# Tile outputs summed six jobs behind their request instead of four, with 15 buffers for them instead of 11

## The chip, the cores and the metric

The kernel runs on one core of one Trainium2 chip. The metric is the device time of one execution in microseconds (us). The kernel before takes 1431.49 us, the median of three runs (1430.09 to 1435.99). The profile was taken from a further execution.

## What is computed

Four layers are applied to 4096 rows of 128 numbers (16 sequences of 256). Each layer adds to its input an attention-like part and a feed-forward part of the normalised input. The change touches the end of layer 0 and the beginning of layer 1. Layer 0's feed-forward part is a mixture of eight experts, cut here to what matters:

```
logits = xn @ gate_w.T;  probs = softmax(logits)
tk_probs, tk_idx = top_k(probs, 2);  tk_probs /= sum(tk_probs) + EPS
out = swiglu(xf, shared)
for e in range(8):
    out = out + w[:, e:e+1] * swiglu(xf, Wg[e], Wu[e], Wd[e])    # w: the two weights, else 0
x = x + ssm(xn) + out
xn = layernorm(x)            # then layer 1: causal attention with 16 heads, and a SwiGLU
```

So each row needs the outputs of two experts, weighted and added.

## The kernel before

**Layout.** The 4096 rows are eight blocks `X[0..7]` of four tiles of 128 rows; a tile has a row in each partition. `HALVES` are the blocks 0 to 3 and 4 to 7; within a half a tile has the number n from 0 to 15.

**Routing and scattering.** Rows are sorted by expert through DRAM. Each row gets two slots in a tensor `XS` of 40 tiles of 256 slots. POOL (GpSimd) writes the rows there with 64 indirect DMAs (L449), 32 for each half: "scatters" below. The first half's rows fill only the tiles below `FIRST` = 24; the second half fills up tiles and takes the rest.

**The jobs.** The loop at L797 takes 40 jobs, k = 0 to 39, one for each tile of 256 slots. Job k fetches weights and slots six jobs ahead on SP's queue (L618, L625), transposes the slots on PE (L636) and evicts them on ACT (L638), two jobs ahead. One job ahead it does the two up-projections (PE tiles `sg` and `su`), SiLU on ACT (L648) and their product on DVE (L649). Then it does the down-projection (PE tile `sy`), evicts it on DVE (L660) and stores it to `YS` in DRAM on SP's queue (L661). PE, ACT, DVE, SP and POOL run in the order in which this block is written (`manual_schedule`); POOL's instructions that are written after the block are merged into its queue when the program is built. The order of the jobs is such that after job 23 all slots of the first half have their outputs.

**Fetching and summing.** From job 24 on, `fetch_outputs(0, n)` (L665) asks for the outputs of one tile of the first half: two indirect DMAs on POOL (L668), "gathers" below, into two tiles `yk` of 64 KB. The dictionary `asked` (L795) says which job asks for which n: 24 for 0 and 1; 25 for 2; 26 for 3; 27 for 4 and 5; 28 for 6; 29 for 7; then one a job up to n = 11 at job 33. `combine(0, n)` (L673) multiplies both by the row's weights and adds them to `X` with two DVE instructions (L678). It stands at the end of the job four behind the request (L811), after that job's L660. All `yk` tiles go round 11 buffers, so that gather number j (0 to 63 in order) waits for the sum that read gather j - 11.

**The first norms.** When output 7 is summed, blocks 0 and 1 are complete, and `norm_steps` (L179) for them is put on the list `norms`. Each job from then on takes one step: statistics of block 0; statistics of block 1 and, on POOL, the scale (`inv_std`, L123 and L124); normalisation of block 0 (DVE, L148); its transposition (PE, L157) and copy (ACT, L194); the same two steps for block 1. When output 11 is summed, the norm of block 2 is appended. What is left when the jobs end is done then (L819).

**Behind the jobs.** The outputs n = 12 to 15 of the first half and all 16 of the second form the list `left` (L827). Six of them are requested at once (12 gathers). The rest follow in `rest()` (L831), a generator that layer 1's attention calls between its own steps: each call sums two outputs and requests two more, and after every fourth output it runs the norm of the block. The second half's outputs need all of `YS`, so the last store too. POOL also issues the load of `pk1i`, weights of layer 1 (L89).

**Layer 1's attention** (`attention`, L850) starts with `project` of block 0, whose matmuls (PE tiles `pq`, `pk`, `pv`) stand behind the last of those norms in PE's order, then the scores `sc`, their maxima on DVE (L952), the weights `se` and the context `av`.

Of the kernel before, what the change touches and what calls it, by code (L numbers as in the profile page):

```python
# [10 lines left out]
F32 = mybir.dt.float32  # L11
# [8 lines left out]
P = 128  # L20
B, S, D = 16, 256, 128
# [34 lines left out]
def program(ctx: ExitStack, tc: tile.TileContext, x, consts, consts0, rows, pk0, w0s, w0e, pk1, pk1i, pk2, pk3, out):  # L56
    nc = tc.nc

    cp = ctx.enter_context(tc.tile_pool(name="keep", bufs=1))
# [119 lines left out]
    def norm_steps(pool, blocks, layer, into=None):  # L179


        n = len(blocks) * NT
        mv = pool.tile([P, n, 2], F32, tag="mvs", name=f"mv{layer}_{blocks[0]}")
        for k, i in enumerate(blocks):
            stats(pool, X[i], mv[:, k * NT : (k + 1) * NT, :], f"st{layer}_{i}")
            if i == blocks[-1]:
                r = inv_std(pool, mv, n, f"r{layer}_{blocks[0]}")
            yield
        for k, i in enumerate(blocks):
            t = into(i) if into else pool.tile([P, NT, D], F32, tag="xn", name=f"xn{layer}_{i}")  # L190
            normalise(t, X[i], mv, r, k * NT)
            yield
            ps = transpose4(t, f"xnT{layer}_{i}")
            nc.scalar.copy(xT[i], ps)  # L194
            yield


    with early, banks(8, 0), tc.tile_pool(name="l0", bufs=2) as sp:
# [21 lines left out]
        for spans in (((0, E), (E + SURE, E + MOST)), ((E + MOST, E + MOST + 8), (E + MOST + 8, TILES))):  # L220
            fills.append([])
            for a, b in spans:
                n = (b - a) * SLOTS // P
# [220 lines left out]
        def at_rows(idx):  # L444
            return bass.IndirectOffsetOnAxis(ap=idx, axis=0)
# [158 lines left out]
        def fetch_weights(k):  # L604
            p = jobs[k] - E
            w = live.setdefault(k, {})
            t = sp.tile([P, 8, 128], F32, tag="blk", name=f"we{k}", bufs=8)
            w["w"] = t[:, 0:6, :]
            for a, b in ((0, SURE), (SURE, WHOLE)):
                if p != a:  # L610
                    continue
                _, values = nc.values_load_multi_w_load_instructions(
                    rows_of[0:1, a:b], engines=[mybir.EngineType.SP], min_val=0, max_val=(E - 1) * P,
                    skip_runtime_bounds_check_because="an expert's number, at most the last one's, times 128",
                )
                experts.update(zip(range(a, b), values))
            of = w0e[bass.ds(experts[p], P), :] if p >= 0 else w0e[(p + E) * P : (p + E + 1) * P, :]
            nc.sync.dma_start(out=w["w"].rearrange("p a b -> p (a b)"), in_=of)  # L618

        def fetch_slots(k):  # L620
            t = jobs[k]
            needs = scatters[0] if k < SURE else scatters[0] + scatters[1]
            assert len(scatters[0]) == 2 * HN and len(scatters[1]) == 2 * HN
            xs = live.setdefault(k, {})["xs"] = sp.tile([P, SLOTS // P, D], F32, tag="xs", name=f"xs{k}", bufs=8)
            d = nc.sync.dma_start(  # L625
                out=xs, in_=XS[rows_in(t), :].rearrange("(t p) d -> p t d", p=P)
            )
            for s in needs:
                tc.add_manual_dep(d.ins, s.ins.name, sync, reason="slots filled")
            return d  # L630

        def turn_slots(k):
            v = live[k]
            ps = bank(f"xsT{k}")
            for t in range(SLOTS // P):
                nc.tensor.transpose(ps[:, t * P : (t + 1) * P], v["xs"][:, t, :], ident)  # L636
            v["xT"] = sp.tile([P, SLOTS], F32, tag="xsT", name=f"xsT{k}", bufs=3)
            nc.scalar.copy(v["xT"], ps[:, 0:SLOTS])  # L638

        def up_slots(k):  # L640
            v = live[k]
            pg, pu = bank(f"sg{k}"), bank(f"su{k}")
            for c in range(2):
                mm(pg[:, c * SLOTS : (c + 1) * SLOTS], v["w"][:, c, :], v["xT"])
            for c in range(2):
                mm(pu[:, c * SLOTS : (c + 1) * SLOTS], v["w"][:, 2 + c, :], v["xT"])
            h = v["h"] = sp.tile([P, 2 * SLOTS], F32, tag="hs", name=f"hs{k}", bufs=3)
            nc.scalar.activation(h, pg, AF.Silu)  # L648
            nc.vector.tensor_tensor(h, h, pu, ALU.mult)  # L649

        def down_slots(k):
            v, to = live.pop(k), jobs[k]
            py = bank(f"sy{k}")
            for t in range(SLOTS // P):
                for c in range(2):
                    o = c * SLOTS + t * P
                    mm(py[:, t * P : (t + 1) * P], v["h"][:, o : o + P], v["w"][:, 4 + c, :], c == 0, c == 1)

            ys = (sp, cp)[k >= NJ - 2].tile([P, SLOTS // P, D], F32, tag="ys", name=f"ys{k}", bufs=3 if k < NJ - 2 else 2)
            nc.vector.tensor_copy(ys, py[:, 0:SLOTS].rearrange("p (t d) -> p t d", d=D))  # L660
            return nc.sync.dma_start(out=YS[rows_in(to), :].rearrange("(t p) d -> p t d", p=P), in_=ys)  # L661

        fetched = {}

        def fetch_outputs(hf, n):  # L665
            for k in range(2):
                y = fetched[hf, n, k] = cp.tile([P, D], F32, tag="yk", name=f"yk{hf}_{n}_{k}", bufs=11)
                nc.gpsimd.indirect_dma_start(  # L668
                    out=y, out_offset=None, in_=YS[0 : FIRST * SLOTS, :] if hf == 0 else YS[:, :],
                    in_offset=at_rows(slots[:, hf, k, n : n + 1]),  # L670
                )

        def combine(hf, n):  # L673
            i = HALVES[hf][n // NT]
            x = X[i][:, n % NT, :]
            for k in range(2):
                m = top[k][:, hf * HN + n : hf * HN + n + 1]
                nc.vector.scalar_tensor_tensor(x, fetched.pop((hf, n, k)), m, x, ALU.mult, ALU.add)  # L678

        def mixed(i):  # L680
            po = bank(f"po0_{i}")
            for t in range(NT):
                mm(po[:, t * P : (t + 1) * P], yT[:, t % 2, 2 * i + t // 2, :], mix, t == 0, t == NT - 1)
            xf = X[i].rearrange("p t d -> p (t d)")
            nc.vector.tensor_tensor(xf, xf, po, ALU.add)
# [101 lines left out]
        with tc.manual_schedule(engines=ordered | {mybir.EngineType.Pool}):  # L787
            for k in range(AHEAD):
                fetch_weights(k)
                fetch_slots(k)  # L790
            for k in range(2):
                turn_slots(k)
            up_slots(0)
            norms = []
            asked = {FIRST: (0, 1), FIRST + 1: (2,), FIRST + 2: (3,), FIRST + 3: (4, 5), FIRST + 4: (6,), FIRST + 5: (7,)}  # L795
            asked.update({FIRST + 6 + n: (8 + n,) for n in range(4)})
            for k in range(NJ):  # L797
                if k + AHEAD < NJ:
                    fetch_weights(k + AHEAD)
                for n in asked.get(k, ()):  # L800
                    fetch_outputs(0, n)
                if k + AHEAD < NJ:
                    fetch_slots(k + AHEAD)
                if k + 2 < NJ:
                    turn_slots(k + 2)
                if k + 1 < NJ:
                    up_slots(k + 1)
                if k % 2 == 0 and 1 <= k // 2 <= NBLK:
                    mixed(k // 2 - 1)
                stored = down_slots(k)  # L810
                for n in asked.get(k - 4, ()):  # L811
                    combine(0, n)
                    if n == 7:
                        norms.append(norm_steps(sp, (0, 1), 1, again))
                    if n == 11:
                        norms.append(norm_steps(sp, (2,), 1, again))
                if norms and next(norms[0], True):
                    norms.pop(0)
            for f in norms:  # L819
                for _ in f:  # L820
                    pass
# [6 lines left out]
        for hn in left[:6]:  # L828
            fetch_outputs(*hn)

        def rest():  # L831
            waiting = left[6:]
            for k in range(0, len(left), 2):
                for hn in left[k : k + 2]:
                    combine(*hn)
                    if waiting:
                        fetch_outputs(*waiting.pop(0))
                yield
                done = left[k + 1]
                if done[1] % NT == NT - 1:  # L840
                    yield from norm_steps(fp, (HALVES[done[0]][done[1] // NT],), 1)
# [818 lines left out]
```

## Time and profile before

| | us |
|---|---|
| median of the runs | 1431.49 |
| the profiled execution | 1435.41 |
| its span, first to last instruction | 1433.6 |
| PE busy (share of the span) | 1267.3 (88%) |
| DVE busy | 774.9 (54%) |
| ACT busy | 561.4 (39%) |
| POOL busy | 344.8 (24%) |
| the 64 gathers, from first to last | 287.5 to 495.4 |
| the 40 jobs' last eviction (L660) begins | 343.66 |
| mean granted clock of TensorE | 0.94 |

The lines of a timeline have the start, the duration, the engine, the line of the kernel, the operation, the tile written and the tiles read, shapes, and in brackets the engine's idle time before and what ended it. PE is the matmul, PEld the load of weights. Groups of the page have the number of instructions behind an x, then busy time and mean duration in ns, then the idle time before them.

### The profile page before, as it was taken

To read this page: it belongs to the slowest core of one execution; us is meant where nothing else is said; L and a number is where in the kernel's file an instruction comes from. 1 tells how busy PE (TensorE), PEld (TensorE's weight loads), DVE (VectorE), ACT (ScalarE), POOL (GpSimd) and SP (SyncE) were. 2 spreads that over 40 slices of the span, in tenths; PEclk is the share of its full clock that TensorE was granted. 3 is DMA by queue.
4 is the path that set the end of the run, shared out by engine and by line. 5 is a ranking of instruction groups with operands and counts; after the bars stand their busy time and mean duration, and the time that the engine had idled before them with its cause. 6 is when DMAs were issued, how large, how long until landed. Compare 5 with 4: busy or idle time off the path is not lost.

```text
span 1433.6 us, 27549 instructions
## 1 busy us (share of the span) xinstructions
PE 1267.3 (88%) x11630; PEld 812.5 (57%) x11630; DVE 774.9 (54%) x1587; ACT 561.4 (39%) x868; POOL 344.8 (24%) x512
## 2 busy tenths in 40 slices
PE   3733699987889999999899999999998999999896
PEld 2512469975555566666545555455555666667434
DVE  7422254435756677767446433554337666567267
ACT  4400122323334544453334433444234555553552
POOL 2456100064312100001012211222112444434012
PEclk9656799998889999999999999999999999999998
DMA  6922575874100000000000000000000000000002
GB/s 195 306 88 74 154 238 170 245 208 149 53 13 16 11 2 3 2 2 2 1 0 0 1 0 0 1 1 0 0 0 2 2 2 2 2 2 2 2 1 59
DMA packets 66731, 72.12 MB, mean 50 GB/s; under 512 B 7344, under 2 KB 57008, under 8 KB 66096
## 3 DMA queue, kind: packets, MB, share of 16 engines
q1 hardware_dynamic: 61936, 60.62, 13.7%
q0 software_dynamic: 4240, 8.99, 2.0%
q8 instruction: 92, 1.51, 0.4%
q10 hardware_dynamic: 432, 0.75, 0.2%
q14 instruction: 31, 0.25, 0.1%
HBM read 52.45 MB, written 17.89 MB: 49 GB/s over the span
## 4 chain that ended last, share of the span: by engine, by line
PE 78%; DVE 12%; issue 6%; ACT 3%; another core or an unknown queue 1%; POOL 0%; DMA 0%; ACTq 0%; DVEq 0%; POOLq 0%
PE h L117 15%; PE sc L117 9%; PE se L117 7%; PE po L117 6%; PE av L117 5%; DVE M L952 4%; PE c L117 3%; PE sy L117 3%; PE sg L117 3%; PE mT L967 2%; PE su L117 2%; PE cv L117 2%; PE pq L117 2%; PE pk L117 2%; PE a L117 1%
## 5 line engine op out<-in xcount | busy, mean ns | idle before, releaser
L952 DVE TENSOR_REDUCE M<-sc 128x4 f32<-128x1024 f32 (+3 forms) x256 | 196.1, 819 | 107.6 <-PE sc L117 98.9
L117 PE MATMUL h<-h,pk 128*128 128x512 f32 x512 | 221.6, 592 | 0.0
L997 ACT ACTIVATE E<-se 128x1024 f32<-128x1024 f32 (+1 forms) x192 | 158.9, 880 | 77.3 <-PE se L117 76.9
L117 PEld LDWEIGHTS h<-h,pk 128*128 128x128 f32 x512 | 96.4, 190 | 117.2 <-issue 115.0
L1004 POOL TENSOR_SCALAR_AFFINE_SELECT E<-E 64x256 f32<-64x256 f32 x240 | 100.5, 419 | 140.5 <-ACT E L997 129.0
L117 PE MATMUL se<-Q,Km 32*128 32x256 f32 (+3 forms) x2048 | 124.0, 336 | 9.9 <-DVE M L952 6.6
L117 PE MATMUL sc<-Kp,Qm 32*128 32x256 f32 (+3 forms) x2048 | 124.3, 338 | 3.0 <-DVE M L952 1.5
L117 PEld LDWEIGHTS sc<-Kp,Qm 32*128 32x128 f32 x2048 | 94.3, 192 | 57.3 <-issue 30.7
L668 POOL DMA_INDIRECT yk<-YS,slots x64 | 61.8, 965 | 248.6 <-DMA we<-in_w0e 135.9
L117 PEld LDWEIGHTS se<-Q,Km 32*128 32x128 f32 x2048 | 88.8, 188 | 48.8 <-issue 34.9
L123 POOL TENSOR_TENSOR v_r<-mv,power 128x4 f32<-128x4 f32 (+1 forms) x23 | 5.2, 226 | 441.1 <-DVE mv L144 441.1
L1243 ACT ACTIVATE h<-h,pk 128x512 f32<-128x512 f32 x64 | 44.0, 687 | 140.8 <-PE h L117 140.7
L117 PE MATMUL cv<-toe,Z 128*32 128x128 f32 x512 | 38.1, 346 | 55.6 <-issue 49.6
L1253 DVE TENSOR_TENSOR x<-x,po 128x512 f32<-128x512 f32 x8 | 5.5, 688 | 139.2 <-PE po L117 139.2
L117 PE MATMUL av<-E,vals 128*32 128x256 f32 (+3 forms) x2048 | 77.2, 301 | 3.8 <-ACT c L1293 1.5
L1022 ACT COPY cu<-av 128x512 f32<-128x512 f32 x32 | 18.8, 586 | 143.5 <-PE av L117 130.3
L449 POOL DMA_INDIRECT XS<-xn,slots x64 | 62.1, 970 | 49.4 <-issue 34.4
L117 PEld LDWEIGHTS av<-E,vals 128*32 128x32 f32 x2048 | 52.7, 110 | 25.0 <-ACT c L1293 2.4
L117 PEld LDWEIGHTS cv<-toe,Z 128*32 128x32 f32 x512 | 23.9, 193 | 68.1 <-issue 61.7
L649 DVE TENSOR_TENSOR hs<-hs,su 128x512 f32<-128x512 f32 x40 | 27.5, 687 | 58.5 <-PE su L117 50.3
L148 DVE TENSOR_SCALAR xn<-x,mv,r 128x128 f32<-128x128 f32 x100 | 46.8, 532 | 14.2 <-POOL r L124 14.1
L117 PE MATMUL sy<-we,hs 128*128 128x128 f32 x320 | 44.2, 283 | 6.9 <-DVE hs L649 6.9
(303 smaller groups left out, 2239.8 us busy)
## 6 DMA issues: line engine op xcount, KB each, us to landing
toe<-kd SPq DMA_DIRECT2D x32, 512.0 KB
we<-in_w0e SPq DMA_DIRECT2D x40, 384.0 KB
xs<-XS SPq DMA_DIRECT2D x40, 128.0 KB
YS<-ys SPq DMA_DIRECT2D x40, 128.0 KB
pk<-in_pk SPq DMA_DIRECT2D x1, 3145.5 KB
XS<-Z SPq DMA_DIRECT2D x3, 1024.0 KB
x<-in_x SPq DMA_DIRECT2D x8, 256.0 KB
ycd<-yc SPq DMA_DIRECT2D x8, 256.0 KB
```

The source lines that it names most:

```text
L117: nc.tensor.matmul(o, l, r, start=start, stop=stop)
L148: nc.vector.tensor_scalar(dst[:, t, :], src[:, t, :], mv[:, at + t, 0:1], r[:, at + t : at + t + 1], ALU.subtract, ALU.mult,)
L449: d = nc.gpsimd.indirect_dma_start(out=XS[:, :], out_offset=at_rows(slots[:, hf, k, n : n + 1]), in_=xn[HALVES[hf][n // NT]][:, n % NT, :] ...
L649: nc.vector.tensor_tensor(h, h, pu, ALU.mult)
L668: nc.gpsimd.indirect_dma_start(out=y, out_offset=None, in_=YS[0 : FIRST * SLOTS, :] if hf == 0 else YS[:, :], in_offset=at_rows(slots[:, h ...
L952: nc.vector.tensor_reduce(dst, src, AX.X, ALU.max, negate=True)
L967: nc.tensor.transpose(ps[:, T, c * P : (c + 1) * P], negm[bl][:, c, T].rearrange("p g j k -> p (g j k)"), ident)
L997: nc.scalar.activation(E[:, 2 * n : 2 * n + 2, :], se[n][:, :, 0 : 2 * wide], AF.Exp, scale=ISQ)
L1004: nc.gpsimd.affine_select(out=d[r], in_=d[r], pattern=[[0, 2], [0, 2], [1, 64]], compare_op=ALU.is_ge, fill=0.0, base=0, channel_multiplie ...
L1022: nc.scalar.copy(cu, ps.rearrange("p (t q) -> p t q", t=2))
L1243: nc.scalar.activation(hn[:, c, :], ps, AF.Gelu, scale=W2[sn][:, c : c + 1])
L1253: nc.vector.tensor_tensor(xf, xf, po, ALU.add)
```

## The change

```diff
         def fetch_outputs(hf, n):
             for k in range(2):
-                y = fetched[hf, n, k] = cp.tile([P, D], F32, tag="yk", name=f"yk{hf}_{n}_{k}", bufs=11)
+                y = fetched[hf, n, k] = cp.tile([P, D], F32, tag="yk", name=f"yk{hf}_{n}_{k}", bufs=15)
...
                 stored = down_slots(k)
-                for n in asked.get(k - 4, ()):
+                for n in asked.get(k - 6, ()):
                     combine(0, n)
                     if n == 7:
                         norms.append(norm_steps(sp, (0, 1), 1, again))
```

The sum of each of the first twelve outputs moves from the job four behind the request to the job six behind it: outputs 0 and 1 from job 28 to job 30, output 7 from job 33 to 35, output 11 from job 37 to 39. The requests stay at jobs 24 to 33. The list `norms` gets its entries two jobs later. The tag `yk` has 15 buffers, four of 512 bytes a partition more, so that gather j waits for the sum that read gather j - 15. This holds for the outputs of `left` too, which use the same tag.

## The prediction

> **What bounds the kernel now.** I read the chain of waits first: PE holds 78% of the chain that ended last, and in the stretch that this change touches (about 287 to 370 us) it is PE matmuls of the expert jobs, broken by stalls. So I asked next for everything that touches the fetched tiles `yk`.
>
> ```profile
> L668 POOL DMA_INDIRECT yk<-YS,slots x64 | 61.8, 965 | 248.6 <-DMA we<-in_w0e 135.9
> ```
> ```profile
> who waited for it (us, times):
>   POOL yk L668: 96.8, 11
>   PEld sc L117: 0.8, 1
>   ACT hs L648: 0.4, 1
>   PE av L117: 0.3, 1
> ```
>
> The first line is the gather, 64 times, 965 ns each; with the 0.30 us between two of them in the timeline, one every 1.25 us. The second list is who waited for a gather or for the sum that frees its buffer. It is nearly all POOL waiting for a free buffer. No DVE row stands there: no sum of L678 ever waited for its tile. The tightest is output 6, fetched at 307.0 and 308.3 us and summed at 318.5, 10 us later. **So the later sum removes no wait of DVE.** What the extra buffers can move is when POOL issues gathers. The busy time by stages shows why that matters (columns: window, its length, then busy time of PE, PEld, DVE, ACT, POOL; then granted clock, DMA share, GB/s).
>
> ```profile
> 250.00:270.00 20.00, 20.00 (x134) 18.69 (x133) 8.68 (x16) 6.19 (x13) 0.00 (x0) 1.00 0.81 249
> 287.00:292.00 5.00, 5.00 (x35) 4.66 (x34) 1.80 (x3) 1.57 (x3) 3.63 (x4) 1.00 0.90 237
> 292.00:302.00 10.00, 5.10 (x29) 4.10 (x27) 1.11 (x2) 0.97 (x2) 6.87 (x8) 0.99 0.57 171
> ```
>
> Before the gathers PE is full. The first run of 11 gathers starts at 287.46; some 4 us later PE, DVE and ACT all fall to half or less, at a granted clock of 0.99 and a falling DMA share. The rows of DVE give the price (L660 evicts one job, here jobs 24 to 27):
>
> ```profile
> 286.26 0.42 DVE L660 COPY ys<-sy 128x256 f32<-128x256 f32 x1
> 289.10 0.42 DVE L660 COPY ys<-sy 128x256 f32<-128x256 f32 x1
> 293.26 0.42 DVE L660 COPY ys<-sy 128x256 f32<-128x256 f32 x1 [1.46 <-PE sg L117]
> 301.11 0.69 DVE L649 TENSOR_TENSOR hs<-hs,su 128x512 f32<-128x512 f32 x1 [7.42 <-remote]
> 303.21 0.42 DVE L660 COPY ys<-sy 128x256 f32<-128x256 f32 x1 [1.41 <-remote]
> ```
>
> A job takes 2.84 us until the gathers run, then 4.16 and 9.95. The multiplication at 301.11 waits for a matmul that PE began at 292.82; it starts when the eleventh gather ends (301.01). The same is plain in the scatter stage, the other long run of indirect DMAs (32 of them, 54.77 to 95.3 us), in PE's timeline:
>
> ```profile
> 90.33 0.37 PE L117 MATMUL cv<-toe,Z 128*32 128x128 f32 x1 [2.43 <-issue]
> 93.13 0.37 PE L117 MATMUL cv<-toe,Z 128*32 128x128 f32 x1 [2.43 <-issue]
> ...
> 100.13 1.16 PE L117 MATMUL cv<-toe,Z 128*32 128x128 f32 x16 [0.33 <-issue]
> ```
>
> One matmul in 2.8 us while the run lasts and 16 in 1.16 us after it. So a long unbroken run of gathers slows PE from about 4 us after its start until its end. I fit the price from the L660 rows. Jobs 25 to 28 (289.10 to 304.81) take 15.71 against 3 x 2.84 = 8.52: 7.2 lost, run of 13.55 us. Jobs 28 to 31 (to 315.96): 2.6 lost, run of six, 7.2 us. Jobs 31 to 34 (to 330.00): 5.5 lost, run of eight, 9.8 us, part of it a clock of 0.83 afterwards. Jobs 34 to 37 (to 339.71): 1.2 lost, 0.95 of it a wait for POOL's scale, seven gathers in twos and threes. **Price: 0.75 x (length of the run - 4 us)**, which gives 7.2, 2.4, 4.3 and 0, together 13.9.
>
> **The change, part by part.**
>
> *Twelve sums moved two jobs later.* Their 24 instructions (349 ns each) still run on DVE in the loop, which is busy 9 us in 20 there; instructions and DMA bytes stay. Cost 0; PE's jobs cover it. If that cover went, 24 x 0.35 = 8.4 us would show, before as now.
>
> *The norms follow the sums.* `norms` is appended at job 35 instead of 33 and 39 instead of 37, one step per job. Before, the first generator (six steps) ends at job 38, and only the norm of block 2 is left over. Now five steps fit, and job 39 holds the sum of output 11 and the normalisation of block 1. This lies on the path that sets the end:
>
> ```profile
> 343.66 0.42 DVE L660 COPY ys<-sy 128x256 f32<-128x256 f32 x1 [0.91 <-PE sy L117]
> 344.00 0.28 DVE L143 BATCH_NORM_STATS2 st<-x 128x6 f32<-128x128 f32 x1
> ...
> 345.77 0.20 POOL L123 TENSOR_TENSOR v_r<-mv,power 128x4 f32<-128x4 f32 x1 [6.82 <-DVE mv L144]
> ...
> 347.13 1.25 DVE L148 TENSOR_SCALAR xn<-x,mv,r 128x128 f32<-128x128 f32 x4 [1.45 <-POOL r L124]
> 347.33 1.02 POOL L668 DMA_INDIRECT yk<-YS,slots  x1 [0.24 <-issue]
> 347.62 1.29 PE L157 MATMUL xnT<-consts,xn 128*128 128x128 f32 x4 [4.00 <-DVE xn L148]
> ```
>
> PE idles 4.00 us while DVE and POOL make block 2's norm, and attention's projections stand behind that transpose. Now a sum pair (0.73, row at 333.50) and a normalisation (1.11, row at 340.70) come ahead of the row at 344.00: **+1.8**. Block 1's transpose (0.44 of PE at 342.13) leaves the loop for that idle time: **-0.4**.
>
> *POOL's place of the scale.* Behind the `v_r` row at 345.77 wait DVE's normalisation and, through it, PE. It now becomes ready 3.9 us after job 39's eviction instead of 2.0. The gathers that need all stores can start 3.0 us after it (their last semaphore wait ended at 346.62, the next gather at 347.33). If the built order puts none of them ahead, 0; if all seven, 7 x 1.25 = 8.8 less 0.9 of slack, about 8. The trace cannot say; the nearest row has the scale ahead, but there it was ready first. I take half a gather, **+0.6**.
>
> *The runs of gathers in the loop.* A gather waits for the sum of the tile 15 places back (11 before). First run: tiles 0 to 14, 18.5 us, price 0.75 x 14.5 = 10.9. Job 28 then evicts at 289.10 + 8.52 + 10.9 = 308.5 and job 30 at 314.2, where the first sums now stand (before, job 30 evicted at 314.35 too). Second run: tiles 15 to 18 at job 30, 19 and 20 at 31, 21 and 22 at 32, unbroken, 10 us: 4.5. Third: 23 to 26 at job 33, 27 and 28 at 34, 7.5 us: 2.6. Then twos: 0. Together 18.0 against 13.9: **+4.1**. Bounds: if the later runs all break up, only 10.9 is left of the 16.5 measured, -5.6; if the 17 gathers after the first run merge into one of 21 us, 10.9 + 12.9 - 13.9 = +10.
>
> The Trainium skill, SBUF — State Buffer, section "Who interferes with whom", says the reverse of my price: a DMA never contends with a compute engine, and only the port pair shared by DVE and GpSimd does. By it this term would be 0. The rows at 292 and at 90 us differ, PE being slowed most.
>
> *After the loop.* Three gathers (347.33 to 350.88) stood ahead of the tile that waited for a sum until 360.84. Now four more are free: seven, 8.75 us, price 3.6. The chain there holds PE for 1.72 + 1.13 + 1.11 + 1.41 = 5.4 of the 9 us from 348.9 to 358.0, so I count 0.6 of it: **+2.1** (bounds 0 and 3.6). In attention the gates are the same sums four tiles on, so the runs of eight at 360.8 and 391.0 stay. Of the last gathers (485.6 to 495.4) four go: 5.0 us, **-0.7**. POOL's other queue entries there (the `pk1i` load at 350.87) have 60 us to spare. SP's queue is not touched: its order and waits are the jobs'.
>
> *Four buffers more* cost space alone (4 x 512 bytes a partition).
>
> **Sum:** 1.8 - 0.4 + 0.6 + 4.1 + 2.1 - 0.7 = +7.5 us on the profiled execution's 1435.4 (span 1433.6, 1.8 around it). That run lies 3.9 above the median of the runs, 1431.5; I add the 7.5 to the median: **1439.0**.
>
> **The rivals.**
>
> *1. The runs cost by something other than their length* (the loads beside them, the number of gathers, which stays). Only the norms count: 1.8 - 0.4 + 0.6, so 1433.5. For it: the run at 360.8 to 370.7 shows no such loss. Against: the scatter stage, and jobs 34 to 37.
>
> *2. Faster: the later runs break up.* From job 30 on, POOL is let go by two tiles a job (2.5 us of gathers per 2.84 us). If the sums come that evenly, no run lasts 4 us after the first; 10.9 replaces the measured 16.5, -5.6, with +1.4 for the norms and -0.7 at the end: -5, 1426.5; 1421 to 1428 with the spread of the fit. It decides from the point where POOL's gaps after tile 18 exceed about 1 us per pair. For: pairs at 327.8 to 332.2 cost nothing visible. Against: jobs 30 and 33 release four at once.
>
> *3. Slower still: POOL's scale stands behind the gathers* (8 instead of 0.6), or the later runs merge (+10 instead of +4.1): 1443 to 1449.
>
> *4. The change does what its words say and no more:* sums had 10 us and over to spare, so this is rival 1's time.
>
> **How the numbers follow.** About 0.5% (7.2 us) is what a measurement of this kernel can tell from no change. The forecast case (1436 to 1442) gets 0.45, 0.25 of it over 1438.7 and 0.20 under. Rivals 1 and 4 (1431 to 1436): 0.20, all within. Rival 3: 0.22, slower. Rival 2: 0.13, 0.07 of it under 1424.3 and so faster. That makes faster 0.07, same 0.46, slower 0.47. The range from 1426 to 1448 leaves out half of rival 2, the end of rival 3 and what I have not thought of. The forecast case's own range is 1436 to 1442.
>
> **What would show it.** Right: the first run has 15 gathers in a row and jobs 25 to 28 take about 19.4 us; job 30 evicts near 314; the gap between the last L660 and the first projection grows from 5.0 us by about 2; seven gathers follow the last store. Wrong: jobs 25 to 28 unchanged with a longer run (then length is not the cause), any DVE wait for `yk`, or more than one gather between the last store and the scale (rival 3).

## The result, and the profile after

| | before | after |
|---|---|---|
| median of the runs, us | 1432.8 (6 runs, 1430.09 to 1437.62) | 1441.37 (6 runs, 1439.37 to 1445.23) |
| profiled execution, us | 1435.41 | 1440.46 |
| its span, us | 1433.6 | 1438.8 |
| mean granted clock of TensorE | 0.940 | 0.942 |

The ratio is 1.0055, with a 95% interval of 1.0042 to 1.0068: 8.6 us slower between the medians. The two profiled executions differ by 5.1 only, since that of before lies 2.6 above its median and that of after 0.9 below.

POOL still waits for the sums that free its buffers, and still no sum waits for its tile. The list of who waited for `yk`:

```profile
who waited for it (us, times):
  POOL yk L668: 103.0, 12
```

The first run of gathers has 15 now, from 285.5 to 304.1 us. DVE's rows beside it (L660 evicts jobs 25 to 28):

```profile
287.20 0.42 DVE L660 COPY ys<-sy 128x256 f32<-128x256 f32 x1
292.04 0.42 DVE L660 COPY ys<-sy 128x256 f32<-128x256 f32 x1 [2.13 <-PE su L117]
299.98 0.69 DVE L649 TENSOR_TENSOR hs<-hs,su 128x512 f32<-128x512 f32 x1 [7.51 <-remote]
307.00 0.42 DVE L660 COPY ys<-sy 128x256 f32<-128x256 f32 x1 [6.33 <-remote]
308.60 0.42 DVE L660 COPY ys<-sy 128x256 f32<-128x256 f32 x1
```

Jobs 25 to 28 take 21.40 us (15.72 before). The busy time in the same stretch (window, its length, PE, PEld, DVE, ACT, POOL, clock, DMA share, GB/s):

```profile
290.00:304.00 14.00, 7.56 (x39) 6.16 (x36) 1.11 (x2) 0.97 (x2) 10.65 (x12) 0.87 0.48 139
```

PE, DVE and ACT all fall, as before; only POOL is busy. The next place is behind the last job, whose eviction begins at 347.82:

```profile
348.81 1.11 DVE L148 TENSOR_SCALAR xn<-x,mv,r 128x128 f32<-128x128 f32 x4
...
350.86 1.01 POOL L668 DMA_INDIRECT yk<-YS,slots  x1 [6.03 <-DMA YS<-ys]
352.17 0.97 POOL L668 DMA_INDIRECT yk<-YS,slots  x1 [0.30 <-issue]
353.17 0.21 POOL L123 TENSOR_TENSOR v_r<-mv,power 128x4 f32<-128x4 f32 x1
353.53 0.97 POOL L668 DMA_INDIRECT yk<-YS,slots  x1
354.51 1.06 POOL L124 TENSOR_TENSOR r<-v_r,power 128x4 f32<-128x4 f32 x1
355.60 1.18 DVE L148 TENSOR_SCALAR xn<-x,mv,r 128x128 f32<-128x128 f32 x4 [4.08 <-POOL r L124]
356.16 1.16 PE L157 MATMUL xnT<-consts,xn 128*128 128x128 f32 x4 [5.85 <-DVE xn L148]
```

The normalisation of block 1 (348.81) stands where it was expected. But POOL, which waited 6.03 us for the last store, then takes two gathers ahead of block 2's `v_r` and a third between `v_r` and `r`. DVE waits 4.08 us for `r`, PE 5.85 for the normalisation, and the first projection begins at 357.11: 9.29 us behind the last eviction, 5.04 before.

### The profile page after: what moved, and what is told of

The parts are those of the page before. It is cut to its first block, busy times and chain, and to the rows that moved or that the text cites. A ratio compares the mean times of both kernels' runs of the same rounds, so it can differ in the third digit from the quotient of the medians.

```text
span 1438.8 us, 27543 instructions
## 1 busy us (share of the span) xinstructions
PE 1263.7 (88%) x11630; PEld 811.2 (56%) x11630; DVE 775.3 (54%) x1587; ACT 561.5 (39%) x868; POOL 345.1 (24%) x512
## 4 chain that ended last, share of the span: by engine, by line
PE 76%; DVE 13%; issue 6%; ACT 3%; another core or an unknown queue 2%; POOL 1%; DMA 1%; ACTq 0%; DVEq 0%; POOLq 0%
PE h L117 15%; PE sc L117 9%; PE se L117 6%; PE po L117 6%; PE av L117 5%; DVE M L952 4%; PE c L117 3%; PE sg L117 2%; PE su L117 2%; PE sy L117 2%; PE mT L967 2%; PE cv L117 2%; PE pk L117 2%; PE pq L117 2%
## 5 line engine op out<-in xcount | busy, mean ns | idle before, releaser
L117 PE MATMUL se<-Q,Km 32*128 32x256 f32 (+3 forms) x2048 | 121.5, 336 | 13.5 <-DVE M L952 10.9
L148 DVE TENSOR_SCALAR xn<-x,mv,r 128x128 f32<-128x128 f32 x100 | 46.6, 530 | 16.4 <-POOL r L124 16.3
```

What stands on the lines that cost most here:

```text
L117: nc.tensor.matmul(o, l, r, start=start, stop=stop)
L148: nc.vector.tensor_scalar(dst[:, t, :], src[:, t, :], mv[:, at + t, 0:1], r[:, at + t : at + t + 1], ALU.subtract, ALU.mult,)
```

## The experiments

Theories: **L**, the length of an unbroken run of gathers slows PE; **N**, the place of the norms is the whole cost; **C**, each gather costs as much wherever it is; **D**, the gathers share DMA engines with the loads; **P**, POOL is busy with gathers, and what stands behind them in its queue is late. (In the expectation of the run without gathers, P is another theory: that a busy POOL slows the others, whatever it does.)

**Two kinds of chip.** The runs fell into two kinds, which nobody chose; each of the four chips of the experiments was met in one session only, and within a session the kind never changed. The scatter stage (32 indirect DMAs; columns as above) shows the difference. The kernel before on the chip of the first pair:

```profile
54.00:100.00 46.00, 18.37 (x113) 10.69 (x105) 10.25 (x39) 3.67 (x6) 31.11 (x32) 0.61 0.38 126
```

The same kernel, profiled again in the second session:

```profile
54.00:100.00 46.00, 34.42 (x280) 25.17 (x280) 28.70 (x98) 7.59 (x13) 33.45 (x33) 0.75 0.63 194
```

POOL does the same work; PE does twice as much beside it, and the whole kernel takes 1348.65 us instead of 1432.8. Below, "first kind" and "second kind"; a ratio is always to the kernel before on the same chip. The first and second session below fell on the second kind, the third and fourth on the first; it was another chip each time.

### First session (second kind; the kernel before 1349.12 us)

**One part alone: the buffers.**

```diff
-... name=f"yk{hf}_{n}_{k}", bufs=11)
+... name=f"yk{hf}_{n}_{k}", bufs=15)
```

> The buffers alone: 15 of them, sums still four jobs behind. Theory L (the length of an unbroken run of gathers slows PE): the first run has 15 gathers as in the changed kernel, so jobs 25 to 28 take about 21 us instead of 15.7, and the gap from the last L660 to the first projection stays at 5.0 us, because the norms are back in their place. The attention behind it keeps what the changed kernel won there (5 us at its sixth sequence). Together +1 to +5 us over the kernel before. Rival N (the place of the norms is the whole cost): no more than the kernel before, and faster by the 5 us of the sixth sequence if those belong to the buffers.

Measured: 1353.09 us, ratio 1.0032 (1.0019 to 1.0046).

**The other part alone: the later sums.**

```diff
-                for n in asked.get(k - 4, ()):
+                for n in asked.get(k - 6, ()):
```

> The lag alone: sums six jobs behind, 11 buffers. POOL has two gathers ahead of the scale of block 2, and a third inside it. Theory L: jobs 25 to 28 take 15.7 us as in the kernel before (a run of 11); the gap from the last L660 to the first projection is 8 to 9.5 us instead of 5.0; together +3 to +5 us. Rival N: the whole +8 us of the changed kernel is here.

Measured: 1349.25 us, ratio 1.0008 (0.9997 to 1.0019).

**Gathers held back.** A gather of the first twelve outputs may not start before the job ahead of its request has been stored.

```diff
-                nc.gpsimd.indirect_dma_start(
+                d = nc.gpsimd.indirect_dma_start(
...
+                if behind:
+                    tc.add_manual_dep(d.ins, behind.ins.name, sync, ...)
...
-                    fetch_outputs(0, n)
+                    fetch_outputs(0, n, stored)
```

> The kernel before, with each gather of the first twelve outputs held until the store of the job before its request: the same 24 gathers, two to four at a time. Theory L: no run over 5 us in jobs 25 to 37, so these jobs lose 0 to 4 us instead of 16.5; 10 to 15 us faster, about 1420 us (0.990 to 0.993). Rival C (each gather has its price, whatever its neighbours): the same time within 2 us. Rival D (gathers cost because they share the DMA engines with the job's loads): the same time or slower.

Measured: 1349.22 us, ratio 1.0001 (0.9989 to 1.0013). L's gain is absent, but the edit spaced nothing out: in its trace 29 gathers still stand in one unbroken run, from 232.57 to 268.75 us, as in the kernel before on this kind (29, 232.79 to 268.96). So this run tests neither L nor C.

**No gathers in the loop.** The first 24 gathers become pairs of POOL fills, 1.04 us a pair where a gather takes 1.25. The kernel leaves out the outputs that they would have fetched: zeros are summed in their place.

```diff
+                if hf == 0 and n < 12:
+                    nc.gpsimd.memset(idle, 0.0)
+                    nc.gpsimd.memset(y, 0.0)
+                    continue
```

> The kernel before, without the gathers of the first twelve outputs: POOL writes zeros in their tiles instead, after a filler of about a gather's length (0.95 us), at the same places of its queue. It leaves out those outputs from the sums. Theories L and C: jobs 25 to 37 lose almost nothing, about 15 us faster (0.989). Rival P (a busy POOL slows the others, whatever it does): jobs 25 to 28 lose some 7 us as before, and the time stays.

Measured: 1341.67 us, ratio 0.9953 (0.9934 to 0.9972): 7.4 us, half of what L and C expected.

*What follows.* On this kind L, C and D have no room. In the run with 15 buffers, 32 gathers stand in one run of 40 us, and the evictions beside it stay 2.83 to 3.18 us apart (jobs 24 to 35). What stops there is DVE, at job 35:

```profile
269.55 1.12 DVE L148 TENSOR_SCALAR xn<-x,mv,r 128x128 f32<-128x128 f32 x4 [9.96 <-POOL r L124]
```

It waits 9.96 us for POOL's scale of blocks 0 and 1, and PE waits with it: theory P. With the fills the same wait is 0.87:

```profile
241.96 0.20 POOL L671 MEMSET yk<- 128x128 f32 x1 [102.43 <-DVE x L683]
...
261.88 0.21 POOL L123 TENSOR_TENSOR v_r<-mv,power 128x8 f32<-128x8 f32 x1
...
263.88 1.20 DVE L148 TENSOR_SCALAR xn<-x,mv,r 128x128 f32<-128x128 f32 x4 [0.87 <-POOL r L124]
```

The fills were not where the gathers had been, though. They wait for no slots, so that 11 of the 24 tiles had been filled by 26.2 us, and POOL idles for 102.43 us before it goes on at 241.96. It therefore comes to the scale early, and the jobs 25 to 39 take 39.70 us, where the kernel before takes 46.50 on this kind: 6.8 of the 7.4. The run says what POOL's queue of gathers costs here. Whether a POOL that is busy with something else slows PE it does not say.

### Second session (second kind; the kernel before 1348.65 us)

**The change, unaltered.**

> The changed kernel, unaltered, because the two chips met so far differ: on the chip of the first pair PE is busy 18 of the 46 us from 54 to 100 us (beside 32 scatters), on the chip of the four runs with one edit each 34 of 46. Theory L (a long run of gathers slows PE, and the first run grew from 11 to 15 gathers): on a chip of the first kind +8 us, ratio 1.0055, jobs 25 to 28 in 19 to 22 us. On a chip of the second kind L has no room (a run of 32 gathers there left the evictions 2.85 us apart), and theory P is left (POOL's 1.25 us a gather is itself the bound, and POOL's scale stands in the queue behind the gathers): +4 to +6 us, the sum of the 4.3 that the buffers alone cost and the 1.1 that the later sums alone cost there, or less where the two stalls are the same stall.

Measured: 1350.72 us, ratio 1.0017 (1.0008 to 1.0027). That is 2.1 us more, under P's 4 to 6 and so in its last clause: the two stalls are the same stall, and the later sums shorten it.

**The kernel before, for its trace.**

> The kernel before, for a trace on the same chip as the others. On a chip of the first kind it repeats the known trace (jobs 25 to 39 in 54.6 us, last eviction to first projection 5.0 us). On a chip of the second kind theory P expects the evictions 2.85 us apart until DVE waits for POOL's scale L124 at about job 35, where one interval is 8 to 12 us; theory L expects no such wait of DVE for POOL.

Its single time was 1350.37 us. POOL's and DVE's rows at job 35:

```profile
268.01 0.94 POOL L668 DMA_INDIRECT yk<-YS,slots  x1 [0.30 <-issue]
268.98 0.22 POOL L123 TENSOR_TENSOR v_r<-mv,power 128x8 f32<-128x8 f32 x1
269.28 1.68 POOL L124 TENSOR_TENSOR r<-v_r,power 128x8 f32<-128x8 f32 x1
...
270.99 1.27 DVE L148 TENSOR_SCALAR xn<-x,mv,r 128x128 f32<-128x128 f32 x4 [6.80 <-POOL r L124]
```

The statistics were complete at 262.6 us; POOL came to the scale at 268.98, behind its 29th gather, having taken one every 1.25 us since 232.8. As P expected. The number of gathers that the program's order puts ahead of that scale sets the wait: 29 before, 32 with 15 buffers. Three more are 3 x 1.25 = 3.75 us, and the wait grew by 9.96 - 6.80 = 3.16. The later sums want the scale two jobs later: with them alone the wait is 3.71, with both parts 4.69. What they gain in the loop they lose behind it: from the last eviction to the first projection, 9.41 and 9.34 us with the later sums, 5.03 and 4.94 without.

**The scale on DVE**, 12 short instructions instead of POOL's two.

```diff
-                r = inv_std(pool, mv, n, ...)
+                r = (on_dve if into and layer == 1 else inv_std)(pool, mv, n, ...)
...
+    def on_dve(pool, mv, n, name):
+        v = pool.tile([P, n], F32, tag="rvar", name=f"v_{name}")
+        nc.vector.tensor_scalar(v, mv[:, :, 1], EPS, None, ALU.add)
+        return inv_sqrt(pool, v, n, name)
```

> The changed kernel with the scale of the two norms in the loop computed on DVE (12 short instructions in place of POOL's two), so that no norm waits for POOL's queue of gathers. Theory P: the wait of DVE for POOL's scale goes. On a chip of the second kind that is 6 to 10 us less than the changed kernel, and faster than the kernel before; on a chip of the first kind the gap from the last eviction to the first projection goes from 9.3 to about 6 us, 3 us less than the changed kernel, ratio about 1.003. Theory L: nothing beyond that gap on either chip; on the second kind 0 to 4 us.

Measured: 1346.16 us, ratio 0.998 (0.9971 to 0.9989): faster than both kernels, 4.6 us less than the change, under P's 6 to 10, since the 12 instructions (269.61 to 271.92) now hold up DVE's own work for the jobs: that job's interval is still 5.6 us. The profiled execution is the slowest of the 12 (1353.12 us). From job 25's eviction to the first projection it takes 48.70 us where the change takes 53.69; what it loses lies ahead of that stretch (3.6 us) and behind the second attention layer's first maxima (3.6). Line numbers are five higher in this kernel (L153 is the former L148). DVE's rows have no wait left:

```profile
272.52 0.42 DVE L665 COPY ys<-sy 128x256 f32<-128x256 f32 x1
273.50 1.11 DVE L153 TENSOR_SCALAR xn<-x,mv,r 128x128 f32<-128x128 f32 x4
```

**The change with gathers held back** (the edit of the first session on the changed kernel).

> The changed kernel with each of the first 24 gathers held back until the job before its request has been stored, so that gathers can't bunch at the first request. Theory L: on a chip of the first kind the first run of 15 breaks up, jobs 25 to 28 fall from 21.4 to under 14 us and the total by 5 to 12 us; on a chip of the second kind no change within 2 us, since runs cost nothing there. Theory P: on either chip no gain, POOL being the bound once gathers have begun; a later start can cost up to 3 us.

Measured: 1353.32 us, ratio 1.0026 (1.0012 to 1.0039): nothing gained. Again the edit spaced nothing out: 32 gathers stand in one run, 232.37 to 272.36 us, and the first starts 1.15 us behind job 24's eviction, in the change 1.31. The 2.6 us over the change are neither a later start nor clear of noise, as the two intervals overlap.

### Third session (first kind; the kernel before 1431.58 us)

**Six buffers.**

```diff
-... name=f"yk{hf}_{n}_{k}", bufs=11)
+... name=f"yk{hf}_{n}_{k}", bufs=6)
```

> The kernel before with six buffers instead of 11, so the other way than the change; sums still four jobs behind. POOL's built order then has 24 gathers ahead of the scale of blocks 0 and 1 (29 before, 32 after the change) and none of the three that wait for the last store ahead of block 2's. Theory P (gathers queued ahead of the scale): on the chips of the eight runs so far DVE's wait for the scale near job 35 falls from 6.8 us to under 1, and the total by 4 to 7 us, ratio 0.995 to 0.997. Theory L (length of the run): nothing there, or 1 to 3 us slower as the gathers come later; on a chip of the first pair's kind the runs of 11, 6 and 8 become one of 6 and then pairs, and the total falls by 6 to 12 us. Rival: with so few buffers a sum waits for its tile, which shows as DVE L678 waiting for yk, 2 us or more slower.

Measured: 1429.20 us, ratio 0.9975 (0.996 to 0.9989). Faster, but by 2.4 and not by 6 to 12. The first run is six gathers, 7.24 us; the next two did not become pairs, as L had it, but stay six and eight (7.19 and 9.73 us). Jobs 25 and 28:

```profile
286.41 0.42 DVE L660 COPY ys<-sy 128x256 f32<-128x256 f32 x1
...
296.01 0.42 DVE L660 COPY ys<-sy 128x256 f32<-128x256 f32 x1 [0.32 <-PE sy L117]
```

9.60 us, against 8.52 without gathers: 1.1 lost. Jobs 25 to 39 take 48.86 us, 5.7 less than before. It is given back later: 1.65 between the first projection and the first sequence's maxima, 4.9 over attention, mostly in the two sequences beside the gathers at 478.7 to 492.2 (23.0 and 24.3 us, 22.5 and 21.6 before). Two waits of DVE for a tile `yk` (2.1 us) are new. The profiled execution is the slowest of 11 (1433.20 us), and in its trace attention gives back more than the jobs gain.

**POOL's order mended in the changed kernel.** The second half's gathers stand behind block 2's scale; nothing else moves.

```diff
+        xin.append(nc.gpsimd.tensor_tensor(r, v, power[:, 16 : 16 + n], ALU.pow))
...
+                ); behind and tc.add_manual_dep(d.ins, behind.ins.name, order, ...)
...
-            fetch_outputs(*hn)
+            fetch_outputs(*hn, xin[-1] if hn[0] else None)
```

> The changed kernel with POOL's order mended in one place: the gathers of the second half, which wait for the last store, stand behind block 2's scale instead of two ahead of it and one inside it; nothing else moves on any engine. Theory P: the gap from the last eviction to the first projection, 9.3 us in the changed kernel on both kinds of chip, goes back to 5.5 to 6.5 us (the sum and the normalisation at job 39 stay, 1.8 us over the kernel before's 5.0), and the total falls by 2.5 to 4 us against the changed kernel: ratio to the kernel before about 0.999 to 1.000. Theory N (the norms' place itself is the cost): the gap stays over 8 us.

Measured: 1436.33 us, ratio 1.003 (1.0018 to 1.0043), where the change had 1.0055 on the first pair's chip. The rows behind the last eviction (349.55):

```profile
353.32 0.21 POOL L123 TENSOR_TENSOR v_r<-mv,power 128x4 f32<-128x4 f32 x1 [6.78 <-DVE mv L144]
353.61 1.01 POOL L124 TENSOR_TENSOR r<-v_r,power 128x4 f32<-128x4 f32 x1
354.65 1.18 DVE L148 TENSOR_SCALAR xn<-x,mv,r 128x128 f32<-128x128 f32 x4 [1.41 <-POOL r L124]
```

The wait for `r` falls from 4.08 to 1.41, and the gap from 9.29 to 6.62. So 2.7 of the 4.25 us come from POOL's order, and the 1.6 left from the sum and the normalisation at job 39. The ratio itself was expected at 0.999 to 1.000, which starts from the change's 1.0017 on the second kind; on this chip the first run of 15 keeps it up (jobs 25 to 28 in 21.22 us).

### Fourth session (first kind, another chip; the kernel before 1432.3 us)

**Eight buffers** (`bufs=8`, sums four jobs behind).

> The kernel before with eight buffers instead of 11. On a chip of the first pair's kind theory L has by now three lengths for the stretch of jobs 25 to 28: runs of 7.2, 13.5 and 18.6 us lost 1.1, 7.2 and 12.8 us, close to the length less 6 us; eight gathers are a run of 9.8 us, so 3 to 5 us lost there, and 2 to 4 us less in all than the kernel before if nothing is given back. On a chip of the other kind the first run costs nothing; theory P: POOL's order has 26 gathers ahead of the scale of blocks 0 and 1 instead of 29, so DVE's wait near job 35 falls from 6.8 us to 2 to 4 us and the total by 2 to 4 us.

Measured: 1430.73 us, ratio 0.9991 (0.9978 to 1.0004), 1.6 us and not distinct from nothing. Jobs 25 and 28:

```profile
288.16 0.42 DVE L660 COPY ys<-sy 128x256 f32<-128x256 f32 x1
...
300.04 0.42 DVE L660 COPY ys<-sy 128x256 f32<-128x256 f32 x1 [0.23 <-PE sy L117]
```

11.88 us, 3.4 lost, as L expected. 2.2 of the gain go again at jobs 37 to 39 (6.18 us instead of 3.95), beside a run of six gathers from 330.4 to 338.0 (before there are three, over ahead of job 37).

**Six buffers in the loop, nine others behind it.**

```diff
-... tag="yk", name=f"yk{hf}_{n}_{k}", bufs=11)
+... tag="yl" if behind else "yk", name=f"yk{hf}_{n}_{k}", bufs=9 if behind else 6)
...
-            fetch_outputs(*hn)
+            fetch_outputs(*hn, xin[-1 if hn[0] else -2])
```

The gathers of the later outputs also stand behind the scale on POOL (`xin` is the list of scales).

> The version that the runs point to: six buffers for the 12 outputs fetched in the loop, nine others for the later outputs, whose gathers stand on POOL behind the scale of blocks 0 and 1 (behind block 2's for the second half); sums four jobs behind, PE, DVE, ACT and SP in the order of the kernel before. Six buffers alone gained 5.7 us in jobs 25 to 39 on a chip of the first pair's kind and gave 5 to 6 us back in attention, whose first gathers then had six buffers too. Theories L and P together: the gain in the loop stays (within 2 us, as the run at its end is eight instead of six) and attention gives nothing back: 3 to 7 us faster than the kernel before on that kind, ratio 0.995 to 0.998. On the other kind the wait for the scale goes (6.8 us to under 1): 5 to 7 us faster, ratio 0.995 to 0.996. Rival: what attention gave back was not the buffers' doing, and the ratio stays at 0.9975 or over on the first kind.

Measured: 1430.13 us, ratio 0.9983 (0.9971 to 0.9995): 2.2 us faster, under the 3 to 7 expected and not better than six buffers for all. Attention gives nothing back this time (712.8 us from the first sequence's maxima to the second attention layer's first; 714.0 before, 718.9 with six buffers throughout). That goes against the rival's reason, though its condition on the ratio (0.9975 or over) is met. But the eight gathers behind the scale (329.6 to 339.5) stand beside jobs 37 to 39, which take 7.15 us.

**The loss against the length of the first run**, first kind, jobs 25 to 28 less 8.52 us:

| buffers | run, us | lost, us | jobs 28 to 37, us |
|---|---|---|---|
| 6 | 7.24 | 1.1 | 34.75 |
| 6 (and nine) | 7.28 | 1.0 | 34.79 |
| 8 | 9.76 | 3.4 | 34.78 |
| 11 (before) | 13.55 | 7.2 | 34.89 |
| 15 (after) | 18.55 | 12.9 | 34.68 |
| 15, order mended | 18.47 | 12.7 | 36.50 |

The loss is the length less about 6.2 us, within 0.6. This holds for the first run alone: the later runs of six and eight gathers (7.2 and 9.8 us) cost 2.6 and 5.5 us in jobs 28 to 34 of the kernel before, and 2.6 and 5.4 with six buffers, where the rule would give 1.0 and 3.6. The stretch behind the first run does not answer to the buffers (the last row, 1.8 us longer, has the same buffers as the one above it).

## Why the prediction was right, and where its steps were off

The time (1439.0, for 1441.37) and the sign held; the sum of +7.5 stands beside +8.6 between the medians and +5.1 between the traces. The two costs that it named, the longer first run and the norms and scale behind the last job, are there, and both are larger than it said. That the sum still comes out close is in part luck: the steps err by 4.9 us in all in the one direction and by 7.2 in the other. By its own steps, from the traces:

| step | predicted | measured |
|---|---|---|
| up to job 25's eviction | 0 | -1.9 |
| first run (jobs 25 to 28) | +3.7 (10.9 for 7.2) | +5.7 (12.9 for 7.2) |
| later runs (jobs 28 to 37) | +0.4 | -0.2 |
| jobs 37 to 39 | -0.4 | +0.6 |
| last eviction to first projection | +2.4 (1.8 + 0.6) | +4.25 |
| on to the first sequence's maxima | +2.1 | +0.7 |
| on to the second attention layer's first maxima | -0.7 | -4.0 |
| behind it | 0 | 0.0 |
| sum | +7.5 | +5.1 |

- *The price of a run.* Mechanism right on chips of the first kind, size off: 0.75 x (length - 4) was fitted on one long run and three shorter ones that other things disturb; for the first run the experiments give 1.0 x (length - 6.2), but not for the later ones. The reading that the stalled multiplication starts when the run ends was wrong: at 299.98 it starts 4.1 us before the end. Nor do the rows show that it waits for a matmul: they put its release down to "remote".
- *The scale behind gathers.* This is the step that failed most in proportion: "half a gather, +0.6". Two gathers stood ahead of `v_r` and one inside the scale, and the mended order shows 2.7 us. It is rival 3's mechanism, at a third of its price, and the prediction's own sign of it, more than one gather between the last store and the scale, came true. The trace of before could not give the order in which the gathers stand.
- *The norms.* 1.8 predicted, 1.6 left when the order is mended.
- *After the loop.* Seven gathers did follow the last store, but cost 0.7 instead of 2.1; the first five of them began before the first projection (the fifth at 357.07), in time that PE lost to the scale anyway. The load of `pk1i`, said to have 60 us to spare, has 44 (DVE reads it at 395.2 in the kernel before); it cost nothing.
- *The last gathers.* Four fewer from 485.6 us on were counted as 0.7. The sequence beside them falls from 22.48 to 17.43 us. On the second kind the same sequence takes 17.43 with five gathers and with one, so the 5 us go with the gathers, though not by their number: with eight beside it the sequence takes 20.11 us (eight buffers) and 22.96 (six). The clock holds part of it: in the kernel before it fell to 0.74 and 0.61 in the second half of that sequence, and stayed at 1.00 after the change.
- *The first 1.9 us* stand ahead of the change and are chance: in the traces of the first kind, job 25's eviction lies between 286.41 and 289.69 us, in kernels that are the same up to there.

The rule of the Trainium skill (SBUF — State Buffer, section "Who interferes with whom"), by which a DMA never contends with a compute engine, was weighed against the rows and set aside. The runs divide it. On the second kind PE is busy 27 of 27 us beside 23 of the change's gathers, as the rule has it:

```profile
231.00:258.00 27.00, 27.00 (x175) 25.07 (x174) 14.88 (x34) 9.10 (x19) 20.30 (x23) 1.00 0.92 271
```

On the first kind a run of them leaves PE 7.56 of 14 us.

**Open.** What makes the two kinds: as each chip was met in one session, it may be the chip or something else that lasted for a session. Whether the run's length or its number of gathers counts: they moved together. Whether POOL's issue, the descriptors or the rows' traffic holds PE: on the second kind POOL's rows are the same and PE runs on, so it is not POOL's work alone. What PE waits for is not seen: in the scatter stage (54 to 100 us of the kernel before) 23.6 us of its waits are put down to "issue", which is nothing that the profile shows. Against D on the first kind stands that the DMA engines are not full beside the gathers (share 0.57 before, 0.48 after), but no run tests it there. Theory C is not settled on the first kind either: in the trace of the change, four gathers more in the first run cost 5.7 us, and four fewer beside attention's sixth sequence save 5.0, and fewer buffers made the whole kernel faster by 2.4 us at most, though the jobs gained up to 5.7. Against C are the pairs of gathers at jobs 33 to 35: these jobs take 3.2 us each in the kernel before on both kinds, so pairs cost nothing there. Each part of the change alone, and no gathers at all, were measured on the second kind only; that the buffers make the longer run on the first kind rests on the row of 6, 8, 11 and 15. The version with the scale on DVE was not run on the first kind, nor six buffers on the second, so no version is shown to be the best on both.

## What to carry to other kernels

More buffers for a gather whose data nobody waits for buy nothing; they let its queue run further ahead, and what stands behind it on that queue pays, and on the first kind what runs beside it too. Read who waits for the tile first, then what short instruction shares its queue and who waits for that one. And before a fit is trusted, vary its one variable: four buffer counts gave the price of the first run that one trace had only suggested. Last, see in the trace whether an edit did what it was for: the gathers that were to be held back ran on in one piece, and 11 of the 24 fills ran some 200 us ahead of their place.

## What the runs showed of the hardware

- The same program took 1432 us in three sessions and 1349 us in two. The two kinds differ where indirect DMAs run: beside 32 scatters PE is busy 18.4 of 46 us on the one and 34.4 on the other, and in the kernel before the time from the second sequence's maxima to the third's, with eight gathers beside it, is 28.0 us on the first kind and 17.1 on the second. Of the 85 us between the two traces of the kernel before, 55 are there by job 25's eviction, 8 come in jobs 25 to 39 and 24 in the first attention layer. Where no indirect DMA runs the two agree: a job takes 2.84 us on both.
- On the first kind the first run of gathers costs nearly its whole length beyond 6.2 us; on the second kind 32 in a row leave the jobs 2.83 to 3.18 us apart.
- The granted clock can differ between executions by more than the waits explain. In the change's first attention sequence on the second kind it is at half from 312 to 316 us, where the kernel before has 1.00, and the sequence takes 20.34 us instead of 17.41:

```profile
312.00:314.00 2.00, 2.00 (x6) 0.49 (x10) 0.04 (x1) 1.93 (x3) 0.00 (x0) 0.50 0.00 0
```

PE waits 1.58 us for maxima ahead of it, and 1.01 in the kernel before. But with 15 buffers alone, and with the gathers of the kernel before held back, that wait is 0.71 us, and the clock is 0.50 for 12 us and the sequence takes 19.85 and 19.93 us. So the longer wait is not shown to be the cause, and single traces of this kind can differ by some 3 us for the clock alone.
